# One-hot matrices kept in DRAM, and a last layer that fetches its source rows by indirect transfer

## The chip, the cores and the metric

The kernel runs on one core of one Trainium2 chip. The metric is the device time of one execution in microseconds, measured without the profiler; 27495.0 us is the median of three runs before the change. Times of stages and instructions come from one further execution that the hardware profiler recorded.

The core's engines run side by side and meet at semaphores: PE (matrix products; its weight loads are counted as PEld), DVE (vector operations), ACT (activations and copies), POOL (simple elementwise work, and the issue of indirect transfers) and SP (issue of ordinary transfers). A product written with fp32 operands is carried out as two passes, which the trace shows as two records.

## What is computed

Four graph layers over 12500 nodes of 16 features and 412500 edges (`src`, `dst`, a type of eight, 16 edge attributes), each followed by a residual and a layer norm:

```python
m = segment_sum(einsum('emh,eh->em', A[edge_type], x[src]), dst)      # layer 0, then a GRU cell
m = segment_sum(einsum('ei,eio->eo', x[src], efeat @ We + be), dst)   # layer 1
h = segment_sum((x[src] @ W[edge_type]) * norm, dst) + x @ root + b   # layer 2, twice (2a, 2b)
# layer 3: both ends of an edge are mixed and their messages are added at both ends
xs, xd = x[src], x[dst]
reflection = lambda a, b: relu(concat([a, b]) @ W1.T + b1) @ W2.T + b2
F_s, F_d = householder(reflection(xs, xd)), householder(reflection(xd, xs))
L_sd = -einsum('eki,ekj->eij', F_s, F_d)
coef = deg_inv_sqrt[src] * deg_inv_sqrt[dst]
msg_s = coef * einsum('eij,ej->ei', L_sd, xd)
msg_d = coef * einsum('eji,ej->ei', L_sd, xs)
out = relu(x - zeros.at[src].add(msg_s) - zeros.at[dst].add(msg_d))
```

Everything is fp32 at the interface. Layer 3 needs, for every edge, the row of its source and of its target, each plain and scaled by the node's inverse root degree (`dis`).

## The kernel before

**Sorting.** `sorted_path` first writes a record of 20 numbers per edge (place of the target in its block, place of the source in its block, a three-bit code `lo`, type, attributes) into a DRAM table `rb`, with 3223 indirect transfers of 128 records each (L1158), and counts degrees with one-hot products meanwhile. After that the edges lie in 100 blocks of targets (`NDB`, 125 nodes each), and within a block in 13 cells by group of sources (`NS`), two to four tiles of 128 edges each, 39 tiles (`TB`) in all. All later stages go through these 1300 cells in order.

**The pipeline of a layer.** `Layer.run` goes through the cells, one iteration per cell, and calls three stages on three neighbouring cells: the first stage on cell i, the second on cell i-1, the third on cell i-2. `prepare` asks at fixed cells of a block for what the next blocks need (records at cell 3, the column arrays `hi` and `lo` at cell 0, one-hots of sources at cells 8 to 10), and `after` puts work into later iterations. Every engine executes its part in the order in which it was written; nothing reorders it. All ordinary transfers of a layer are issued by SP.

The first stage gathers source rows on PE: `gather` multiplies the node table, split in three bf16 parts, by a one-hot of the source's place (L1264), and DVE keeps the right eighth of the result with `lo` (L1266). It also makes the one-hots of targets: `targets` has POOL compare, tile by tile, a row of 0 to 124 with each edge's place (L1275) and write a 128 x 125 fp32 matrix. The second stage folds the gathered rows (products with `fold`, L1346, L1489) and multiplies them by type or attribute on DVE (L1358, L1492). The third adds them up over the block's edges with the one-hot of targets as an operand of an fp32 product (L1382, L1506). So layers 0, 1, 2a and 2b each make the same 3900 target matrices anew, in four buffers `target`.

In layer 2a, `by_type` is also given `dis_tab`: beside each gather a further product fetches the sources' `dis` values (L1334), ACT copies them (L1339), PE turns them (L1349) into the same PSUM tile as the folded rows, ACT copies that part out (L1354), and at the end of a block DVE selects and stores them in `dis_e` (L1397 to L1402). Layer 3 reads `dis_e`.

**Layer 3.** `rows3` gathers the source rows as above and makes, on POOL, a second one-hot `to_d` the other way round (L1666). `hidden` forms the hidden layer for both directions with two fp32 products 128 to 512 columns wide (L1685, L1686) and a Relu on ACT. `ends` turns things back to one edge per partition with three products per tile (second weight matrix, source row, scaled target row; L1698 to L1700) and copies them out. Once a block is complete, `reflections` computes its two Householder reflections in fourteen steps over the whole block, two of them on POOL (L1731, L1732), the others mostly on DVE. After that come the sums: `put_cell` makes one-hots `from_s` of the source's place on POOL and adds the messages to the source's accumulators (L1791); `put_block` makes all 39 target one-hots of the block in one iteration and adds up the messages at the targets (L1801):

## Time and profile before

| | us |
|---|---|
| runs before, median (lowest, highest) | 27495.0 (27483.48, 27551.82) |
| profiled execution, its own time | 27450.57 |
| span of its instructions | 27448.7 |
| busy: PE, PEld | 23153.0, 19061.4 |
| busy: DVE, ACT, POOL | 14425.5, 2855.9, 20842.0 |
| granted TensorE clock, mean | 0.853 of full |
| moved by DMA | 1347.76 MB, 49 GB/s over the span |

A busy engine is one with an instruction under way; for PE, whose products overlap in a pipeline, that is more than its work at full rate. The stages stand one after another in the trace: the sort and its preparation until 5296 us, layer 0 until 8080, layer 1 from 8097 to 11535, layer 2a from 11590 to 16001, layer 2b from 16020 to 18600, layer 3 from 18650 to 27410; small node-wise steps lie between them. The clock is what the chip grants TensorE over time; in this trace it is either full or half, so a mean of 0.82 over a stage says that about a third of the stage ran at half clock.

In the lists of groups, a line gives engine, operation, what is written and read, sizes and count; then the busy time in us and the mean of one in ns; then the idle time of the engine just before these instructions, and what ended it.

### The profile page before, as it was taken

The page shows a single profiled execution, that of the slowest core. Times are in us where ns is not written, and L with a number is a line of the kernel's source. Part 1 is how long each engine was busy: PE and PEld are TensorE (multiplying, and loading weights), DVE is VectorE, ACT ScalarE, POOL GpSimd, SP SyncE. Part 2 cuts the span into 40 slices and gives each one's busy share as a digit, 9 for nine tenths or more (in the row PEclk, how much of TensorE's full clock was granted, in tenths as well). Part 3 has the DMA queues.
Part 4 walks back from the last instruction along what each step waited for, and adds up shares of the span by engine and source line. Part 5 has one row for each costly group of instructions (what it writes and reads, how often), then busy time and mean ns, then how long its engine had stood idle before and what let it go on. Part 6 is the DMA issues. An engine that isn't in the chain of part 4 may idle for free.

```text
span 27448.7 us, 382621 instructions
## 1 busy us (share of the span) xinstructions
PE 23153.0 (84%) x143679; PEld 19061.4 (69%) x143679; DVE 14425.5 (53%) x31460; ACT 2855.9 (10%) x8264; POOL 20842.0 (76%) x28149
## 2 busy tenths in 40 slices
PE   1666400299999999999999999998999999999998
PEld 0444300288878888777777778887888888888887
DVE  7999700166666666644444466664334344344433
ACT  0000000000001111122211200001111111111111
POOL 3888777798876666555554579996888888888888
PEclk9999855599999999987776799998888888888887
DMA  2000111133322222211111123331111111111100
GB/s 81 12 12 12 13 15 15 35 92 85 84 75 68 68 68 68 58 58 54 51 51 48 54 75 91 91 91 39 33 35 35 35 35 35 35 35 35 34 31 23
DMA packets 799013, 1347.76 MB, mean 49 GB/s; under 512 B 537098, under 2 KB 588689, under 8 KB 732485
## 3 DMA queue, kind: packets, MB, share of 16 engines
q1 hardware_dynamic: 676142, 1268.61, 16.6%
q0 software_dynamic: 103136, 33.21, 0.8%
q8 instruction: 1150, 18.84, 0.3%
q10 hardware_dynamic: 17883, 21.35, 0.2%
q14 instruction: 702, 5.75, 0.1%
HBM read 1245.07 MB, written 77.79 MB: 48 GB/s over the span
## 4 chain that ended last, share of the span: by engine, by line
PE 69%; POOL 18%; DMA 5%; issue 4%; DVE 3%; ACT 0%; another core or an unknown queue 0%; SPq 0%; POOLq 0%; ACTq 0%; DVEq 0%
POOL rb L1158 13%; PE g L1264 11%; PE acc L1382 10%; PE x L1346 8%; PE g L1801 8%; PE acc L1506 7%; DMA rec<-rb 4%; PE acc_s L1791 4%; PE hid_ps L1685 3%; PE hid_ps L1686 3%; PE ends_ps L1700 3%; PE ends_ps L1699 3%; POOL target L1275 3%; PE ends_ps L1698 3%; PE x L1489 3%
## 5 line engine op out<-in xcount | busy, mean ns | idle before, releaser
L1275 POOL TENSOR_SCALAR target<-iota_f,rec 128x125 f32<-128x125 f32 x19500 | 11698.1, 624 | 3872.9 <-PE acc L1382 2537.4
L1266 DVE SCALAR_TENSOR_TENSOR masked<-lo,part_lo,g 128x384 f32<-128x384 uint8 (+2 forms) x6500 | 3991.1, 614 | 8807.2 <-PE g L1264 8759.7
L1264 PE MATMUL g<-oh,table 125*128 125x384 bf16 (+2 forms) x19500 | 4635.2, 349 | 124.7 <-DVE oh L1245 124.3
L1158 POOL DMA_INDIRECT rb<-rec,at x3223 | 3692.2, 1146 | 1074.0 <-issue 981.8
L1382 PE MATMUL acc<-target,pr 128*128 128x125 f32 x23400 | 3962.1, 310 | 0.0
L1346 PEld LDWEIGHTS x<-fold,masked 128*128 128x128 f32 x23400 | 3377.5, 210 | 512.4 <-issue 268.4
L1346 PE MATMUL x<-fold,masked 128*128 128x16 f32 x23400 | 3337.7, 270 | 16.0 <-DVE masked L1266 16.0
L1382 PEld LDWEIGHTS acc<-target,pr 128*128 128x128 f32 x23400 | 3266.2, 211 | 35.6
L1275 POOL TENSOR_SCALAR from_s<-iota_f,rec 128x125 f32<-128x125 f32 x3900 | 3263.2, 855 | 11.4 <-PE acc_s L1791 10.6
L1358 DVE TENSOR_TENSOR pr<-x,w 128x384 f32<-128x384 f32 (+2 forms) x3900 | 2172.6, 557 | 1385.2 <-ACT d_e L1354 1282.4
L1264 PEld LDWEIGHTS <-table 125*128 125x128 bf16 x19500 | 2025.6, 105 | 934.9 <-issue 242.3
L1172 PE MATMUL cnt_ps<-in_col,in_row 128*125 128x400 bf16 x6446 | 1608.9, 330 | 915.4 <-DVE in_col L1147 600.7
L1801 PE MATMUL g<-msg,target 128*125 128x16 f32 x7800 | 2249.5, 379 | 1.0 <-POOL target L1275 0.3
L1666 POOL TENSOR_SCALAR to_d<-jd,part 125x384 f32<-125x384 uint8 (+2 forms) x1300 | 1678.7, 1291 | 746.0 <-PE ends_ps L1700 637.9
L1801 PEld LDWEIGHTS g<-msg,target 128*125 128x125 f32 x7800 | 1926.7, 308 | 323.9 <-POOL target L1275 3.9
L1506 PE MATMUL acc<-pr,target 128*125 128x272 f32 x7800 | 2106.5, 406 | 0.0
L1045 PE MATMUL tp<-ident,x_rows 125*128 125x125 f32 x13 | 5.6, 462 | 2053.5 <-DMA x_rows<-in_x 2051.3
L1172 PEld LDWEIGHTS <-in_row 128*125 128x125 bf16 x6446 | 857.9, 133 | 1261.7 <-issue 643.6
L1698 PEld LDWEIGHTS ends_ps<-w,hid 128*128 128x128 f32 x7800 | 1323.1, 196 | 389.8 <-issue 119.2
L1506 PEld LDWEIGHTS acc<-pr,target 128*125 128x125 f32 x7800 | 1364.8, 188 | 216.9 <-issue 0.3
L1791 PE MATMUL acc_s<-placed,from_s 128*125 128x128 f32 x7800 | 1306.8, 305 | 219.2 <-POOL from_s L1275 209.5
L1699 PE MATMUL ends_ps<-fold,masked 128*128 128x16 f32 x7800 | 1483.5, 266 | 0.0
(301 smaller groups left out, 28568.6 us busy)
## 6 DMA issues: line engine op xcount, KB each, us to landing
hi<-hi_d SPq DMA_DIRECT2D x500, 1218.8 KB
lo<-lo_d SPq DMA_DIRECT2D x500, 624.0 KB
rec<-rb SPq DMA_DIRECT2D x500, 390.0 KB
jd<-jd_d SPq DMA_DIRECT2D x100, 609.4 KB
rb<-rec,at POOLq DMA_INDIRECT x3223
rec<-in_edge_attr SPq DMA_DIRECT2D x100, 256.0 KB
rb<-null SPq DMA_DIRECT2D x7, 3030.0 KB
rb<-null ACTq DMA_DIRECT2D x6, 3030.0 KB
```

The costliest lines, as they stand in the source:

```text
L1158: put = nc.gpsimd.indirect_dma_start(out=rb, out_offset=bass.IndirectOffsetOnAxis(ap=at[:, t : t + 1], axis=0), in_=rec[:, k, :], in_offse ...
L1172: nc.tensor.matmul(cnt_ps[:NB, h, :NC2], in_row, in_col[:, h * NC2 : (h + 1) * NC2], start=False, stop=False, skip_group_check=True,)
L1264: nc.tensor.matmul(g[:, :w], tab[:NB, s, k, :], self.oh[d][:NB, cols], start=k == 0, stop=k == 2)
L1266: nc.vector.scalar_tensor_tensor(m[:, :w], self.lo[d][:, cols], part_lo, g[:, :w], op0=OP.is_equal, op1=OP.mult)
L1275: nc.gpsimd.tensor_scalar(oh[:, k, :], iota_f[:, :NB], self.rec[d][:, t + k, code : code + 1], None, op0=OP.is_equal)
L1346: nc.tensor.matmul(x[:, k, :D], m[:, k * P : (k + 1) * P], fold, start=True, stop=True)
L1358: nc.vector.tensor_tensor(pr[:, :n], x[:, :n, None, :D].to_broadcast([P, n, R, D]), layer.w8[d][:, t : t + n, :, None].to_broadcast([P, n, ...
L1382: nc.tensor.matmul(acc[:, :NB], pr[:, k].rearrange("p r f -> p (r f)"), oh[:, k, :], start=t + k == 0, stop=t + k == TB - 1,)
L1506: nc.tensor.matmul(acc[:NB, :WE], oh[:, k, :], pr[:, k, :], start=t + k == 0, stop=t + k == TB - 1)
L1699: nc.tensor.matmul(ps[:, k, 2 * D : 3 * D], m[:, here], fold, start=True, stop=True)
L1791: nc.tensor.matmul(acc_s[:NB, s // 4, s % 4, :], oh[:, k, :], placed[:, k].rearrange("p l f -> p (l f)"), start=False, stop=False, skip_gr ...
L1801: nc.tensor.matmul(ps[:NB, :D], oh[:, k, :], msgs[d][:, t + k, 1, :], start=t + k == 0, stop=t + k == TB - 1,)
```

## The change

**Target one-hots are made once.** `targets` becomes `make`, which has POOL make a cell's matrices as before, now in six buffers, and has SP write them to DRAM, and `fetch`, which loads a cell's matrices from DRAM. Layer 0 makes and stores the targets (`to_d`, 100 arrays of 128 x 4875 fp32). Layers 1, 2a and 2b load them, seven cells at the start and then one cell per iteration, six cells ahead, into ten buffers. Layer 1 also makes and stores the one-hots of sources (`from_d`). The stores and loads of a three-tile cell have 192 KB.

**Layer 2a loses the side product**: `dis_tab`, `d24` and `dis_e` go, and so 2a runs the same instructions as 2b.

**Layer 3 is written anew.** A DRAM table `pairs` holds each node's row beside its scaled row, 32 numbers. `fetch_sources` has POOL fetch, per tile, the 128 rows of the edges' sources with one indirect transfer, nine cells ahead, at addresses that DVE computes from the records. The targets' rows, plain and scaled and each in three bf16 parts, come from one product per tile with a bf16 one-hot `to_t` (made by DVE, three operations a block), and DVE adds the three parts. A tile's two rows stand side by side, one transpose per cell turns them (`turn_rows`), and one fp32 product per tile gives the hidden layer (`hidden`). `ends` keeps one product per tile. The sums take both one-hots from DRAM and add target messages cell by cell; POOL makes no one-hots here. `idle` issues products of zeros into a spare part of PSUM: five an iteration of 384 columns, twenty in every 52nd. The loop is written out; the stages of a cell lie one iteration apart, and its sums come 30 iterations after its rows. The loads of `hi` and `lo` and the table go from this layer; `jd` becomes bf16 (1.2 MB a block in place of 0.6).

```diff
+        def make(self, d, t, n, code, to, name):
+            oh = self.work.tile([P, 4, NB], F32, name=name, bufs=6)
             for k in range(n):
                 nc.gpsimd.tensor_scalar(
                     oh[:, k, :], iota_f[:, :NB], self.rec[d][:, t + k, code : code + 1], None, op0=OP.is_equal
                 )
+            nc.sync.dma_start(to[d][:, t * NB : (t + n) * NB], oh[:, :n, :].rearrange("p t j -> p (t j)"))
             return oh
+        def fetch(self, j, of, name="target", bufs=10):
+            d, s, t, n = all_cells[j]
+            oh = self.work.tile([P, 4, NB], F32, name=name, bufs=bufs)
+            nc.sync.dma_start(oh[:, :n, :].rearrange("p t j -> p (t j)"), of[d][:, t * NB : (t + n) * NB])
+            self.fetched[name, j] = oh
...
             while i < n + len(stages) - 1 or any(j >= i for j in self.later):
+                if ahead is not None:
+                    for j in range(0 if i == 0 else i + 6, i + 7):
+                        ahead(j)
...
             def rows(i, d, s, t, n, _):
                 m = layer.gather(d, s, t, n)
-                d24 = None
-                if dis_tab is not None:
...
-                return m, layer.targets(d, t, n), d24
+                if first:
+                    return m, layer.make(d, t, n, 0, to_d, "target")
+                return m, layer.fetched.pop(("target", i))
...
         def rows1(i, d, s, t, n, _):
-            return layer.gather(d, s, t, n), layer.targets(d, t, n)
+            layer.make(d, t, n, 1, from_d, "from")
+            return layer.gather(d, s, t, n), layer.fetched.pop(("target", i))
...
+        def idle(n):
+            for _ in range(n):
+                nc.tensor.matmul(
+                    side[:, :3].rearrange("p b c -> p (b c)"), zeros[:, :P], zeros[:, : 3 * P], start=True, stop=True
+                )
+        def targets_t(d, k):
+            w = TB * P // 3
+            cols, to = to_t[d]
+            here = slice(k * w, (k + 1) * w)
+            nc.vector.tensor_scalar(to[:NB, here], cols[:NB, here], part[:NB], None, op0=OP.is_equal)
+        def fetch_sources(j):
+            d, s, t, n = all_cells[j]
+            if s == 0:
+                ends_of[d] = work.tile([P, TB, 5, D], F32, name="ends", bufs=3)
+            for k in range(t, t + n):
+                nc.gpsimd.indirect_dma_start(
+                    out=ends_of[d][:, k, 2:4, :].rearrange("p k f -> p (k f)"), out_offset=None,
+                    in_=pairs, in_offset=bass.IndirectOffsetOnAxis(ap=at_of[d][:, k : k + 1], axis=0),
+                )
...
+        def rows3(i, d, s, t, n):
+            ps = psum.tile([P, 4, 3 * 2 * D], F32, name="rows_ps", bufs=1)
+            for k in range(n):
+                nc.tensor.matmul(
+                    ps[:, k, :], to_t[d][1][:NB, (t + k) * P : (t + k + 1) * P],
+                    x_parts[d][:NB].rearrange("p k c -> p (k c)"), start=True, stop=True,
+                )
+            return ps
+        def sum_rows(j, ps, d, t, n):
+            x_of[j] = work.tile([P, 4, 2, D], F32, name="x_e", bufs=3)
+            parts = ps[:, :n, :].rearrange("p t (k c f) -> p c t f k", k=3, f=D)
+            nc.vector.tensor_reduce(x_of[j][:, :n, 0, :], parts[:, 0], AX.X, OP.add)
+            nc.vector.tensor_reduce(ends_of[d][:, t : t + n, 4, :], parts[:, 1], AX.X, OP.add)
+            nc.scalar.copy(x_of[j][:, :n, 1, :], ends_of[d][:, t : t + n, 2, :])
...
+        def put(j):
+            d, s, t, n = all_cells[j]
+            placed = put_of.pop(j)
+            to, oh = layer.fetched.pop(("target", j)), layer.fetched.pop(("from", j))
+            sums = acc_s[:, 3].rearrange("p s c -> p (s c)")[:NB, (2 + d % 2) * P : (2 + d % 2) * P + D]
+            for k in range(n):
+                nc.tensor.matmul(
+                    sums, to[:, k, :], msgs[d][:, t + k, 1, :], start=False, stop=False, skip_group_check=True
+                )
...
         with tc.manual_schedule():
-            layer.run([rows3, hidden, ends], prepare3)
+            for i in range(n_cells + late_by):
...
+                fetch_sources(i + LEAD)
+                j = i - late_by + 6
+                if 0 <= j < n_cells:
+                    layer.fetch(j, to_d, bufs=8)
+                    layer.fetch(j, from_d, "from", bufs=8)
...
+                idle(5 if i % (4 * NS) else 20)
```

## The prediction

> **What bounds the kernel now.** I read the page's table and slices first, then a table of windows by stage, then each stage's groups and waits.
>
> ```profile
> span 27448.7 us, 382621 instructions
> ...
> POOL 3888777798876666555554579996888888888888
> ...
> PEclk9999855599999999987776799998888888888887
> ```
>
> No engine bounds the whole: POOL (76% busy) and PE (84%) change places, and the clock granted to PE is below full in the middle and at the end. By stage (sorting, layer 0, layer 1, layer 2a, 2b, layer 3; the columns after the length are busy us of PE, PEld, DVE, ACT, POOL, then clock, DMA share, GB/s):
>
> ```profile
> 0.00:5296.00 5296.00, 1781.83 (x9797) 1311.38 (x9797) 3103.99 (x13050) 84.28 (x442) 3853.45 (x3249) 0.80 0.12 22
> 5296.00:8080.00 2784.00, 2649.83 (x20077) 2399.63 (x20077) 1736.88 (x3047) 105.30 (x437) 2351.00 (x3910) 0.93 0.31 84
> 8097.00:11535.00 3438.00, 3433.05 (x20406) 2797.79 (x20405) 2251.37 (x3003) 352.92 (x1614) 2305.98 (x3887) 1.00 0.24 67
> 11590.00:16001.00 4411.00, 4280.55 (x25073) 3151.60 (x25073) 2013.65 (x3490) 921.85 (x2708) 2419.22 (x3887) 0.76 0.17 52
> 16020.00:18600.00 2580.00, 2468.23 (x19906) 2265.46 (x19907) 1746.87 (x3202) 30.68 (x114) 2361.58 (x3900) 0.98 0.33 90
> 18650.00:27410.00 8760.00, 8506.75 (x48302) 7116.17 (x48302) 3503.77 (x5609) 1327.76 (x2899) 7540.93 (x9300) 0.82 0.11 34
> ```
>
> All but the first run over 100 target blocks, so the lengths are also us per block times 100: 27.8, 34.4, 44.1, 25.8, 87.6. Layer 1 is PE alone (busy 3433 of 3438 at clock 1.00). 2a and 2b compute the same thing from different tables; 2a carries the `d24` side product as well and takes 1.7 times as long, at clock 0.76. Layer 3 is POOL, 7541 of 8760 busy, with one-hot matrices:
>
> ```profile
> L1275 POOL TENSOR_SCALAR from_s<-iota_f,rec 128x125 f32<-128x125 f32 x3900 | 3263.2, 855 | 11.4 <-PE acc_s L1791 10.6
> L1275 POOL TENSOR_SCALAR target<-iota_f,rec 128x125 f32<-128x125 f32 x3900 | 2250.5, 618 | 0.0
> L1666 POOL TENSOR_SCALAR to_d<-jd,part 125x384 f32<-125x384 uint8 x1108 | 1433.7, 1294 | 606.9 <-PE ends_ps L1700 590.5
> ```
>
> In each block `put_block` makes 39 targets in one run of 22.5 us (timeline of POOL) while PE follows at POOL's pace. In 2a the waits are those of the side product, not of POOL, which itself waits for PE:
>
> ```profile
> POOL target L1275 <- PE acc L1382: 1998.9, 1272, 20.2
> DVE pr L1358 <- ACT d_e L1354: 1280.3, 1200, 3.5
> ```
>
> 2b shows PE's own pace at full clock, from one gather to the next (1.82 us for a cell of three tiles):
>
> ```profile
> 17100.63 0.65 PE L1264 MATMUL g<-oh,table 125*128 125x384 bf16 x3
> 17101.12 0.74 PE L1346 MATMUL x<-fold,masked 128*128 128x16 f32 x6
> 17101.71 0.91 PE L1382 MATMUL acc<-target,pr 128*128 128x125 f32 x6
> 17102.45 0.65 PE L1264 MATMUL g<-oh,table 125*128 125x384 bf16 x3
> ```
>
> Each fp32 product is two passes, started 0.112 us apart, whatever its width up to 128 columns; a bf16 one of 384 columns takes 0.163 us.
>
> **The change, part by part.** Against this profile's 27448.7 us (execution 27450.6; the median of the runs, 27495, lies 44 us above).
>
> *2a loses the side product.* 1300 products of L1334, 3900 of L1349, two ACT copies per cell, the wait 1280 us, and the end-of-block work of L1397 to L1402 go. What remains is 2b's program, for which 2b is the row: 2580. PE by its pace: 13 x 1.82 = 23.7 us a block, plus about 1.3 for `by_f` and `node`: 25.0, against POOL's 23.6 now. So 2b was nearly PE-bound already, and freeing POOL in it is worth at most 0.8 us a block, which I give to late transfers. 2a: 4411 to 2600, **-1811**; 2b: 2570, **-10**. The cover is the clock: were 2a granted layer 0's 0.93, it would be 2600/0.93 = 2800.
>
> *Layer 0 stores each target matrix.* POOL still makes 39 a block (23.5). A cell's buffer is now free when PE has used it and its 192 KB store has landed; six buffers replace four. The nearest row for a landing behind other traffic is the column load at 2b's start:
>
> ```profile
> 16022.28 0.34 SPq L1236 DMA_DIRECT2D hi<-hi_d  x1
> ...
> 16035.97 1.78 DVE L1245 TENSOR_SCALAR oh<-hi,part 125x1664 bf16<-125x1664 bf16 x3 [17.55 <-DMA hi<-hi_d]
> ```
>
> 13.7 us from issue to use. By the packet records its 9984 B packets (0.376 us) run on about five of the sixteen DMA engines. The stores stand in SP's queue behind this load once a block, and in the order of instructions each SP transfer also waits for the eighth before it to land. Six cells last 6 x 2.0 = 12 us; a store behind `hi` lands some 16 us after it, so POOL may stall 4 us a block: 0 to +400 us, below nothing too (two more buffers): -100. I take **+120**, as POOL has some slack (23.5 of 27.8). Queued behind SP's wait for POOL are the loads of `rec`, `hi`, `lo`, needed 8 cells later.
>
> *Layer 1 loads targets and stores `from`.* PE-bound; POOL's 39 makes (23.1 of 34.4) and the loads lie beside it; what comes onto SP is 26 issues of 0.33 us. The ten `target` buffers give a load 9 cells x 2.5 = 23 us against 16 us of landing. **+20**; ends 0 and +250 (a queue at 2.5 us a block).
>
> *2a, 2b load targets* beside PE: 9 cells x 1.82 = 16.5 us against the same 16, covered with nothing to spare; if not, +2 us a block each (+400).
>
> *Layer 3.* POOL's 75.4 busy us a block go. What comes onto POOL is 39 indirect gathers a block; before has scatters of the same 128 rows:
>
> ```profile
> 2499.47 1.33 POOL L1158 DMA_INDIRECT rb<-rec,at  x1 [0.30 <-issue]
> ...
> 4000.77 0.96 POOL L1158 DMA_INDIRECT rb<-rec,at  x1 [0.30 <-issue]
> ```
>
> Start to start they come every 1.26 us with VectorE silent and every 1.64 us while VectorE compares without a break. So POOL needs 39 x 1.26 = 49.1 to 39 x 1.64 = 64.0 us a block. VectorE's share: of its work in layer 3 only the long operations with two SBUF operands (L1744, L1751, L1757, L1763, L1765, L1769: 5 x 1.45 + 2 x 0.82 = 8.9 us) and the compares of `targets_t` (3 x 0.65) hold POOL up; overlaps with `from_s` show it: 0.60 us undisturbed, 0.86 on average. By the scatters' rate (0.38 us lost in 1.64) those 10.8 us cost 2.5 us; blocked outright, 10.8. I take 4: **53 us a block**, nearer the scatters, the same instruction.
>
> PE at full clock, per block: `sums`, `acc_s`, `hidden`, `ends` 4 x 39 x 0.224 = 34.9; `turn_rows` 13 x 0.22 = 2.9; `rows3` 39 x 0.08 = 3.1 (between L1349's 0.04 and a 256-column gather's 0.113); dummy products 65 x 0.163 = 10.6: **51.5 us**. DVE: 13 x (`add_bias` 0.2 by L1392, two reductions 0.25 each by L1737's 1.15 ns an element, `at_lo` 0.2, `placed` 0.69) = 20.7, reflections 14.4, compares and small ones 3.5: 38.6. ACT about 15; its copy of a gathered row waits for the gather, and behind it stand the copies and the Relu that PE needs, which nine cells of lead cover. SP takes over 28 issues of 0.33 us, 9 us of a block in which it was idle. DMA: 26 matrices of 192 KB, `jd`, records and rows, 7 MB a block, 130 GB/s over 54 us; 2b moves 90, and three 390 KB record loads at its start ran at 190 (packet records). PE's `put` waits for two transfers, asked for six cells (25 us) ahead. POOL at 53 and PE at 51.5, coupled through nine cells of lead: 54.5 us a block. Ends: 51.5 and 64. Plus start (table `pairs`, first gathers) 45 and the drain of 30 cells at about 2.2 us, 65: 100 x 54.5 + 110 = 5560, **-3200**.
>
> The gap before 2a loses its table, **-15**. Sum: 120 + 20 - 1811 - 10 - 3200 - 15 = -4896: 27451 to 22555. The median stands 0.16% above the profiled execution; with that, **22590**.
>
> Row first, then page: L1275's `from_s` at 855 ns against `target`'s 618 in the same stage is VectorE standing in POOL's way. The Trainium skill, "GPSIMD Engine Reference", Key points, says that POOL shares its SBUF interfaces with VectorE, in contention with two-port modes or two SBUF inputs; by that rule, taken fully, the sum would be 23140 in place of 22590. Row: the sort's scatters of 10 KB follow each other at 1.26 us. Against that speaks the Trainium skill, "DMA: Bandwidth & Descriptors", Anatomy of one DMA: a transfer issued from POOL costs 2.0 us plus its bytes at 436 GB/s. An estimate by it is 2.04 us for a gather of 16 KB, 79.5 us a block were each to wait for the last, and a sum of 25100; the row is below it since eight are in flight, and I go by the row.
>
> **The rivals.**
> 1. *VectorE blocks the gathers*: 49.1 + 10.8 = 60 us a block, 100 x 60 + 110 = 6110, 550 over my term: 23140 (at 64 us: 23540). For it: the `from_s` row. Against it: scatters lost only 0.38 us beside a fully busy VectorE. 14%.
> 2. *Late transfers bind layers 0 to 2*: layer 0 at 32 us (+300 on my term), layer 1 +130, 2a and 2b +2 us a block each (+400): 23420. For it: 13.7 us landings and one queue. Against: DMA share 0.33 at most. 10%.
> 3. *The clock falls*: layer 3 at 0.82, as now, 51.5/0.82 = 62.8 us (+830), 2a at 0.93 (+200): 23620. For it: 2a lost its clock with PE 97% busy. Against: layer 1 and 2b hold 0.98 to 1.00 and layer 3 has no 22 us stretch at POOL's pace left. 8%.
> 4. *Landings pace the gathers, slower than before.* Each gather waits for the eighth before it to land. Landing at 13.7 us means 1.71 us each, 67 us a block (+1230), 23820 (4%). Level with before is reached only when layer 3 takes 8760 + 1696 = 10456, or 103 us a block: 2.65 us a gather, 21 us per landing; past that it is slower. Against it: 1.26 us steady in the sort bounds the landing there by 10 us. 4%.
>
> **How the numbers follow.** The forecast, 60%: 22000 to 23100 (layer 3 at 50 to 58 us, layer 0 at 27 to 30). The rivals as above, the two cases of the fourth together 8%. The range 21900 to 24000 leaves out the slower end of the fourth and tails. Faster by over 0.3% (about what a measurement here can tell from no change) 0.95, same 0.01, slower 0.04.
>
> **What will show it.** 2a's window equal to 2b's within 5%, clock 0.97 or more; layer 1 within 2%; layer 0's POOL waiting for DMA stores, if my +120 is right; in layer 3 POOL's gathers 1.3 to 1.45 us apart, PE busy above 90%, clock near 1.00. Wrong if the gathers come over 1.6 us apart, if PE waits for `target` or `from` transfers, or if layer 2 stays at 40 us a block.

## The result: slower on the chip of the record, and the profile after

The changed kernel took 27992.2 us (median; 27965.5 to 28024.0), beside 27523.4 us for the kernel before in the same series (27483.5 to 27553.3). The ratio is 1.0172, with a 95% interval of 1.0151 to 1.0192. The forecast was 22590 us. The profiled execution took 27974.95 us, its span is 27972.9 us.

The stages (us). So that they add up, each layer is taken from its first gather product (L1264 before, L1267 after) to that of the next layer, and layer 3 from the last gather product of 2b to the end. The forecast is before's length plus the terms of the sum, with the -15 for the gap counted in layer 1. The last column is the same changed kernel on another chip, run at the end of the study:

| stage | before | forecast | after | after, chip 4 |
|---|---|---|---|---|
| sort | 5327 | 5327 | 5329 | 5327 |
| layer 0 | 2769 | 2889 | 3346 | 3341 |
| layer 1 | 3487 | 3492 | 3490 | 3490 |
| layer 2a | 4455 | 2644 | 2596 | 2597 |
| layer 2b | 2552 | 2542 | 2565 | 2570 |
| layer 3 | 8860 | 5660 | **10647** | **5532** |
| span | 27449 | 22553 | 27973 | 22856 |

Layer 3 is the step that failed, by 4987 us on this chip and by 128 us the other way on chip 4. Layer 0 came out 457 and 452 us over the forecast.

The page of the changed kernel, its span and the slices of POOL and of TensorE's granted clock:

```profile
span 27972.9 us, 376773 instructions
...
POOL 3888777667776676710000001333333333333332
PEclk9999855677779999999999999677766666666666
```

POOL is idle through layer 2 and only a third busy in layer 3, the last sixteen slices. The clock, full in layers 1 and 2, falls to 0.6 with layer 3. The table of windows (layers 0, 1, 2a, 2b, 3, with bounds a little within or beyond the stages': those of 2a and 2b open 25 and 54 us after the first gather product; after the length, busy us of PE, PEld, DVE, ACT, POOL, then clock, DMA share, GB/s):

```profile
5296.00:8600.00 3304.00, 3116.79 (x20011) 2806.83 (x20012) 1706.53 (x3002) 91.25 (x417) 2323.77 (x3900) 0.78 0.46 147
8646.00:12110.00 3464.00, 3430.08 (x20404) 2796.13 (x20404) 2271.76 (x3008) 352.44 (x1613) 2382.98 (x3900) 0.99 0.71 211
12190.00:14725.00 2535.00, 2445.66 (x19741) 2245.95 (x19739) 1704.64 (x3171) 30.62 (x114) 0.00 (x0) 0.99 0.72 187
14815.00:17331.00 2516.00, 2427.87 (x19654) 2231.70 (x19652) 1696.96 (x3157) 29.44 (x111) 0.00 (x0) 0.99 0.72 187
17345.00:27930.00 10585.00, 6535.08 (x43447) 5759.16 (x43444) 3543.78 (x9291) 1401.17 (x4206) 3730.65 (x3900) 0.67 0.28 70
```

In layer 3 no engine is near full: PE 62%, DVE 33%, POOL 35%, the DMA engines 28%. So everybody waits. The table of waits of layer 3 (engine, line, whom it waited for: total us, times, longest):

```profile
ACT x_t L1732 <- PE side L1728: 3332.9, 1058, 6.7
DVE ends L1752 <- remote: 2428.2, 138, 41.2
ACT x_t L1732 <- remote: 1740.6, 135, 52.1
...
ACT sum_d L1837 <- remote: 1470.5, 86, 34.9
PE side L1639 <- issue: 1185.3, 138, 41.7
```

"Remote" and "issue" mean that the profile shows nobody who released the wait in time. `add_bias` (L1752) waits for nothing but TensorE's products of L1747, yet 138 of its waits, up to 41 us long, are put down to nobody. The timeline of one such stretch shows why:

```profile
21985.74 0.27 PE L1728 MATMUL side<-ident,x_e 128*96 128x128 f32 x1
...
21986.52 0.53 PE L1747 MATMUL ends_ps<-w,hid 128*128 128x32 f32 x4
...
21989.49 0.94 POOL L1684 DMA_INDIRECT ends<-pairs,at_i  x1 [0.30 <-issue]
21989.75 0.26 ACT L1732 COPY x_t<-side 96x128 f32<-96x128 f32 x1 [6.26 <-remote]
21990.07 0.97 PE L1639 MATMUL side<-zeros 128*128 128x384 bf16 x5 [3.02 <-issue]
21990.74 0.95 POOL L1684 DMA_INDIRECT ends<-pairs,at_i  x1 [0.30 <-issue]
...
21991.01 0.93 PE L1833 MATMUL acc_s<-msg,target 128*125 128x16 f32 x4
...
21997.46 0.23 DVE L1752 TENSOR_TENSOR ends<-ends_ps,b 128x64 f32<-128x64 f32 x1 [9.80 <-remote]
...
22017.07 0.17 ACT L1837 COPY sum_d<-acc_s 125x16 f32<-125x16 f32 x1 [23.08 <-remote]
...
22017.44 1.22 PE L1840 MATMUL acc_s<-placed,from 128*125 128x128 f32 x4 [25.51 <-issue]
```

The transpose L1728 is over at 21986.0, and ScalarE, which waits for nothing but TensorE and its own earlier work, copies it at 21989.75: 3.7 us late. The products of L1747 end at 21987.05 and VectorE takes them at 21997.46, 10.4 us late. Those of L1833 end at 21991.94 and `sum_d` follows at 22017.07, 25 us late. Meanwhile POOL issues a gather every 1.25 us, undisturbed. Each gather is as cheap as hoped; what is late is the news that TensorE is done. TensorE itself has gone on to later products by then (L1639 at 21990.07, L1833 at 21991.01). The ends of products are modelled in these records, though, so results that reach PSUM late would look the same.

The trace also records raises of semaphores. For each recorded raise of TensorE's in layer 3 I took the time since the end of the last product recorded before it, and sorted the raises by how long POOL's run of gathers had been going (a run is 39 gathers, 49 us, then POOL waits some 57 us for the next free `ends` tile):

```
us since the run of gathers began    raises   median lateness us   95th percentile
 0 to 5                                 667         0.01                 0.12
 5 to 10                                291         0.09                 3.23
10 to 15                                164         1.82                 4.43
20 to 25                                 61        11.0                 13.8
35 to 40                                 33        22.8                 26.3
55 to 60                                761         0.01                22.4
65 to 110                              5802         0.01                 0.01
VectorE's raises, all of layer 3       7669         0.01                 0.02 (longest)
```

The lateness grows as long as gathers go and is gone a few us after the run. VectorE's recorded raises are never late. Not every raise left a record: of VectorE's in the first 50 us of the runs, 737 of 1906 did. The waits say the same without these records. Between 5 and 50 us into a run, 89% of TensorE's 222 waits of over 1 us end within 0.35 us of the end of an instruction of ScalarE or VectorE; only 12% of ScalarE's 319 and 35% of VectorE's 317 end so soon after an instruction of the other two. So it is TensorE's news that is late. In the sort, where POOL scatters every 1.26 us, those of TensorE's raises that left a record are 0.02 us late at most; the same holds for layers 0 to 2 (medians 0.01 us, at most 0.02 us in 99% of them). That much the profile of the changed kernel says; what sets it off needed runs.

### The profile page after: what moved, and what is told of

It reads as the page before. It is cut to its first block, busy times and chain, and to the rows that moved or that the text cites. A ratio compares the mean times of both kernels' runs of the same rounds, so it can differ in the third digit from the quotient of the medians.

```text
span 27972.9 us, 376773 instructions
## 1 busy us (share of the span) xinstructions
PE 19864.6 (71%) x133626; PEld 17244.4 (62%) x133626; DVE 14144.4 (51%) x34826; ACT 2023.8 (7%) x6956; POOL 12293.8 (44%) x14949
## 5 line engine op out<-in xcount | busy, mean ns | idle before, releaser
L1684 POOL DMA_INDIRECT ends<-pairs,at_i x3900 | 3730.6, 957 | 11931.5 <-DMA w_h<-in_l_w_t 5300.4
L1269 DVE SCALAR_TENSOR_TENSOR masked<-lo,part_lo,g 128x384 f32<-128x384 uint8 (+2 forms) x5200 | 3192.4, 614 | 3868.1 <-PE g L1267 3769.0
L1382 PE MATMUL acc<-target,pr 128*128 128x125 f32 x23400 | 3850.4, 304 | 0.0
L1267 PE MATMUL g<-oh,table 125*128 125x384 bf16 (+2 forms) x15600 | 3626.6, 343 | 116.2 <-DVE oh L1248 116.2
L1382 PEld LDWEIGHTS acc<-target,pr 128*128 128x128 f32 x23400 | 3214.4, 208 | 0.3
L1840 PE MATMUL acc_s<-placed,from 128*125 128x128 f32 x7800 | 1494.6, 339 | 2088.8 <-issue 1557.8
L1278 POOL TENSOR_SCALAR from<-iota_f,rec 128x125 f32<-128x125 f32 x3900 | 2383.0, 632 | 1106.7 <-DMA from_d<-from 1037.0
L1639 PE MATMUL side<-zeros 128*128 128x384 bf16 x7060 | 1722.2, 387 | 1548.5 <-issue 1185.3
L1278 POOL TENSOR_SCALAR target<-iota_f,rec 128x125 f32<-128x125 f32 x3900 | 2323.8, 615 | 997.5 <-PE acc L1382 635.7
L1840 PEld LDWEIGHTS acc_s<-placed,from 128*125 128x125 f32 x7800 | 1243.2, 236 | 2093.8 <-issue 1559.7
L1752 DVE TENSOR_TENSOR ends<-ends_ps,b 128x96 f32<-128x96 f32 (+2 forms) x1300 | 334.0, 257 | 4066.0 <-remote 2428.2
L1267 PEld LDWEIGHTS <-table 125*128 125x128 bf16 x15600 | 1600.0, 103 | 780.4 <-issue 195.4
L1639 PEld LDWEIGHTS <-zeros 128*128 128x128 bf16 x7060 | 840.7, 131 | 1998.9 <-issue 1799.1
L1739 PE MATMUL hid_ps<-x_t,w_h 96*128 96x128 f32 (+2 forms) x7800 | 1420.4, 331 | 218.2 <-ACT hid L1741 167.4
```

Source lines behind the costliest of these rows:

```text
L1267: nc.tensor.matmul(g[:, :w], tab[:NB, s, k, :], self.oh[d][:NB, cols], start=k == 0, stop=k == 2)
L1269: nc.vector.scalar_tensor_tensor(m[:, :w], self.lo[d][:, cols], part_lo, g[:, :w], op0=OP.is_equal, op1=OP.mult)
L1278: nc.gpsimd.tensor_scalar(oh[:, k, :], iota_f[:, :NB], self.rec[d][:, t + k, code : code + 1], None, op0=OP.is_equal)
L1382: nc.tensor.matmul(acc[:, :NB], pr[:, k].rearrange("p r f -> p (r f)"), oh[:, k, :], start=t + k == 0, stop=t + k == TB - 1,)
L1639: nc.tensor.matmul(side[:, :3].rearrange("p b c -> p (b c)"), zeros[:, :P], zeros[:, : 3 * P], start=True, stop=True)
L1684: nc.gpsimd.indirect_dma_start(out=ends_of[d][:, k, 2:4, :].rearrange("p k f -> p (k f)"), out_offset=None, in_=pairs, in_offset=bass.Indi ...
```

## The experiments

The results name the chip of each group of runs; for the record of the changed kernel itself no chip is named. Layer 3's us a block are the mean distance of the `sum_d` copies (L1837), the last three distances, in which the pipeline drains, left out. "Late" is the share of TensorE's raises in layer 3 over 1 us late; in the changed kernel it is 9.9%, at 104.7 us a block.

### Chip 7: without the gathers, paced, unread, and the other way round

`e1_plain`: the gathers give way to one plain transfer a block.

```diff
                 ends_of[d] = work.tile([P, TB, 5, D], F32, name="ends", bufs=3)
-            for k in range(t, t + n):
-                nc.gpsimd.indirect_dma_start(
-                    out=ends_of[d][:, k, 2:4, :].rearrange("p k f -> p (k f)"), out_offset=None,
-                    in_=pairs, in_offset=bass.IndirectOffsetOnAxis(ap=at_of[d][:, k : k + 1], axis=0),
-                )
+                nc.scalar.dma_start(
+                    ends_of[d][:, :, 2:4, :].rearrange("p t k f -> p t (k f)"),
+                    pairs[: P * TB].rearrange("(t p) c -> p t c", p=P),
+                )
```

> Layer 3 as in the changed kernel, but the 39 indirect gathers of a block are replaced by one plain transfer of the same bytes in the same 128 B pieces, issued by ScalarE; the rows that arrive are not those of the edges' sources, so the sources' terms are left out of the computation. In the changed kernel layer 3 takes 10585 us (105 us a block), and TensorE's semaphore updates come up to 39 us after the recorded end of the product that makes them, only while POOL's gathers run. Theory A (the gathers, as indirect transfers of POOL's own queue, delay what TensorE reports as done): layer 3 falls to 51 to 56 us a block, 5200 to 5700 us, whole kernel about 22900 to 23100, updates on time. Theory B (SP's queue starves TensorE: the loads of the stored one-hot matrices and of the 1.22 MB target columns land late, whoever loads the sources): layer 3 stays at 95 to 110 us a block, whole kernel 27000 to 28000. Theory C (any transfer of 4992 pieces of 128 B a block into SBUF does it): layer 3 also stays above 80 us a block.

22454 us; 49.5 us a block, 0.0% late. The window of layer 3:

```profile
17345.00:22430.00 5085.00, 4952.59 (x43523) 4451.86 (x43523) 3536.47 (x9305) 1415.21 (x4220) 0.00 (x0) 0.99 0.60 145
```

The same products, at clock 0.99 and PE 97% busy: theories B and C fall on this chip. SP's queue, the loads of `target` and `from` and 4992 pieces of 128 B a block hurt nothing here.

`e1_paced`: POOL waits in each iteration for ScalarE.

```diff
             nc.scalar.copy(x_t_of[j][: n * 2 * D], tp[: n * 2 * D])
+            tick[j] = work.tile([P, 1], F32, name="tick", bufs=8)
+            nc.scalar.copy(tick[j][:64], x_t_of[j][:64, :1])
...
+                if i - 2 in tick:
+                    pace = work.tile([P, 1], F32, name="pace", bufs=2)
+                    nc.gpsimd.tensor_copy(pace[:64], tick.pop(i - 2)[:64])
                 fetch_sources(i + LEAD)
```

> The changed kernel with a pace for POOL: each iteration ScalarE copies one column of the turned rows to a small tile, and POOL copies it before it issues that iteration's three gathers, so the 39 gathers of a block come three an iteration instead of 39 in one run of 49 us. Theory A1 (the delay builds only in a long uninterrupted run of gathers: it is under 0.1 us in the first 5 us of a run and over 10 us after 20 us): layer 3 falls to 55 to 65 us a block, whole kernel 23000 to 24200. Theory A2 (each gather costs TensorE its time wherever it stands, about 1.25 us x 39 = 49 us a block on top of 52): layer 3 stays at 95 to 110 us a block, whole kernel 27000 to 28500. Theory B (SP's queue): layer 3 stays too.

23084 us, 55.2 us a block, 0.0% late: as A1 had it. I took this for the cure; the later groups take that reading away.

`e1_unread` and `e1_scatter`: plain transfers as above, and POOL's 3900 transfers into nothing.

```diff
+                    at_fix = work.tile([P, TB], I32, name="at_fix", bufs=1)
+                    nc.vector.tensor_scalar(at_fix, iota_f[:, :TB], float(P), part, op0=OP.mult, op1=OP.add)
...
-                    out=ends_of[d][:, k, 2:4, :].rearrange("p k f -> p (k f)"), out_offset=None,
+                    out=spares[d][:, k, :, :].rearrange("p k f -> p (k f)"), out_offset=None,
```

> As e1_plain (the sources' rows are left out, plain transfers in their place), but POOL issues its 3900 indirect gathers as well, all in one run from the start of layer 3, into tiles that nobody reads and with fixed addresses, so nothing waits for them. They last 3900 x 1.25 = 4875 us; after that layer 3 goes on without gathers, so one run shows both. Theory A (gathers delay TensorE by running, not by being waited for): while they run a block takes 110 us or more, so about 35 to 45 blocks are done in 4875 us, the rest at 51 to 56 us, layer 3 about 7900 to 8700 us, whole kernel 25400 to 26200. Theory D (the stalls come from waiting for the gathered rows): 51 to 56 us a block throughout, layer 3 5200 to 5700, whole kernel about 23000.

> As e1_unread, but POOL's 3900 indirect transfers go the other way: 128 rows of 128 B from SBUF scattered to DRAM rows that nobody reads, as the sort stage does (there TensorE's updates are 0.01 us after the recorded ends, beside 1.26 us scatters). The sources' rows are left out. Theory A as it stands for any indirect transfer: same as e1_unread, layer 3 7900 to 8700 us. Theory A with the direction (only rows that come from DRAM into SBUF delay TensorE): 51 to 56 us a block, layer 3 5200 to 5700 us.

22790 and 22834 us; both 49.5 us a block while gathers or scatters came every 1.37 and 1.38 us, 0.0% late. So a run of indirect transfers need not delay TensorE. Theory A as I had stated it was gone.

### Chip 2: runs without readers, one pace a block, another pace, a fourth buffer

```diff
 e2_bursts_unread (e1_unread with the blocks' own addresses)
-                    in_=pairs, in_offset=bass.IndirectOffsetOnAxis(ap=spares["at"][:, k : k + 1], axis=0),
+                    in_=pairs, in_offset=bass.IndirectOffsetOnAxis(ap=at_of[d][:, k : k + 1], axis=0),
 e2_pace_block (e1_paced, once a block)
-                if i - 2 in tick:
+                if i - 2 in tick and (i + LEAD) % NS == 0:
 e2_pace_dve (the changed kernel, and)
+            at_c = work.tile([P, 4], I32, name="at_c", bufs=4)
+            nc.vector.tensor_copy(at_c[:, :n], at_of[d][:, t : t + n])
...
-ap=at_of[d][:, k : k + 1]
+ap=at_c[:, k - t : k - t + 1]
 e2_ends4 (the changed kernel, and)
-name="ends", bufs=3) ... name="at_i", bufs=3)
+name="ends", bufs=4) ... name="at_i", bufs=4)
```

> As e1_unread (the sources' rows come by plain transfers from fixed rows, so their terms are left out), but the gathers use each block's own addresses, as in the changed kernel, so POOL is held once a block until the addresses of the block after next are made: runs of 39 gathers with a wait between, into tiles that nobody reads. Theory E (a run of 39 gathers that starts after a wait delays TensorE's updates whoever reads them): layer 3 stays at 90 to 110 us a block, whole kernel 26500 to 28000. Theory F (the delay needs somebody who waits for the gathered rows, ScalarE's copy and VectorE's products, beside POOL running ahead): 53 to 57 us a block, whole kernel 22700 to 23100.

> e1_paced with POOL's pacing copy only once a block, ahead of the block's first gather, so the 39 gathers again come in one run of 49 us, nine cells ahead of their use, and are read as in the changed kernel. Theory F or E (the run of 39 is what does it): layer 3 goes back to 90 to 110 us a block, whole kernel 26500 to 28000. Theory G (what matters in e1_paced is that POOL no longer waits for the release of the ends tile itself, not how the gathers are spread): 54 to 57 us a block, about 23100.

> The pace of e1_paced made another way: in each iteration VectorE copies that iteration's three addresses to a small tile of their own, and the gathers read them there, so they wait for VectorE and POOL executes nothing but gathers; ScalarE's extra copy is gone too. If the spreading is what helps: 54 to 57 us a block, whole kernel 22950 to 23150. If it was POOL's copy between the gathers (an instruction of another kind that breaks the run): 90 to 110 us a block, 26500 to 28000.

> The changed kernel with four instead of three buffers for the tile the rows land in, and four for the addresses: POOL no longer waits for the release of the tile but for the addresses, and each run of 39 gathers starts some nine iterations earlier, its rows landing long before ScalarE copies them. Theory H (the runs come too late: ScalarE waits for rows, TensorE behind it, and the loop falls out of step): 55 to 65 us a block, whole kernel 23000 to 24200. Theory E or F (the run of 39 itself): 90 to 110 us a block, 26500 to 28000.

27557, 27992, 25274 and 27695 us; 100.8, 105.3, 77.6 and 101.5 us a block; 9.0, 9.3, 7.8 and 9.8% late. `e2_bursts_unread` says that nobody need wait for the gathered rows (theory F falls) and `e2_ends4` that the runs are not too late (theory H falls). `e2_pace_block` says that one wait of POOL's own does not help (theory G falls). The pace through VectorE helps by half. Its layer 3, window and two waits:

```profile
17345.00:25220.00 7875.00, 7052.27 (x43468) 6170.43 (x43467) 3641.03 (x10587) 1393.20 (x4208) 3876.49 (x3900) 0.71 0.37 94
```

```profile
POOL ends L1686 <- DVE at_c L1684: 1504.2, 508, 7.7
POOL ends L1686 <- DVE ends L1754: 1010.3, 229, 9.1
```

POOL now waits for VectorE in most iterations, so gathers come in threes; PE is busy 7052 us where `e1_plain` needed 4953, at clock 0.71. Compared with `e1_unread`, `e2_bursts_unread` differed in its program only in the addresses and in the wait for them, and so the next runs vary these; that it ran on another chip I left out of account.

### Chip 14: addresses, layout, a copy on POOL, and layer 0

```diff
 e3_unread_rows (e1_unread, and)
-                    nc.vector.tensor_scalar(at_fix, iota_f[:, :TB], float(P), part, op0=OP.mult, op1=OP.add)
+                    nc.vector.tensor_copy(at_fix, at_of[0])
 e3_blockmajor (the changed kernel, and)
-        nc.sync.dma_start(pairs[: P * NPB].rearrange("(p n) c -> p (n c)", p=P), both)
+        nc.sync.dma_start(
+            pairs[: P * NPB].rearrange("(n p) c -> p n c", p=P), both.rearrange("p (n c) -> p n c", c=2 * D)
+        )
...
-                at, layer.rec[d][:, :, 1], float(NPB), eight_s[:, d // LO, :], op0=OP.mult, op1=OP.add
+                at, eight_s[:, d // LO, :], float(P), layer.rec[d][:, :, 1], op0=OP.mult, op1=OP.add
...
-            nc.vector.tensor_add(at_of[d], at, lo_e[d])
+            nc.vector.scalar_tensor_tensor(at_of[d], lo_e[d], float(P), at, op0=OP.mult, op1=OP.add)
 e3_pool_copy (e1_paced without ScalarE's tick)
-                if i - 2 in tick:
+                if i >= 2:
-                    nc.gpsimd.tensor_copy(pace[:64], tick.pop(i - 2)[:64])
+                    nc.gpsimd.tensor_copy(pace[:64], part[:64])
 e3_paced_early (e1_paced, and)
-            if k == 3 and d and d + 2 < NDB:
-                layer.load_records(d + 2)
+            if k == (0 if first else 3) and d and d + 2 < NDB:
+                layer.load_records(d + 2, 4 if first else 3)
```

> e1_unread with one difference: the 3900 unread gathers, all in one run without a wait on another engine, use the addresses of the first block's edges (rows scattered over the table, as in the changed kernel) instead of rows p + 128 k, which lie one behind the other. The sources' rows are again left out of the computation. Theory J (what delays TensorE is a run of gathers of scattered rows; rows in sequence do not do it): while the gathers run TensorE does about 4 cells in 49 us, as inside a run of the changed kernel, so about 30 blocks in 4875 us and 70 blocks at 49 us after: layer 3 about 8300 us (7500 to 9500), whole kernel 24900 to 26900. Theory K (the waits between runs do it, the addresses do not): 49 to 51 us a block as in e1_unread, whole kernel 22700 to 22900.

> The changed kernel with the table of pairs laid out by block (row block x 128 + j instead of j x 104 + block), so the rows of one cell lie in 128 KB instead of being spread over 1.7 MB; runs of 39 gathers as before, no pace. Theory J in the form that nearness is what counts: 50 to 60 us a block, whole kernel 22500 to 23600. Theory J in the form that only rows in sequence are harmless, or theory K: 90 to 110 us a block, 26500 to 28000.

> e1_paced without the pace: POOL copies a constant column before each iteration's three gathers and waits for nobody, so runs of 39 gathers stay, broken every third gather by an instruction of another kind (e2_pace_dve had the pace without the copy: 78 us a block). If the copy is what helps in e1_paced: 54 to 60 us a block, whole kernel 22900 to 23600. If the pace is: 85 to 110 us a block, 26000 to 28000. Both in part: 65 to 85 us a block.

> e1_paced, and in layer 0 the records of the block after next are loaded three cells earlier (ahead of the two column loads, with a fourth buffer). In the changed kernel TensorE waits 175 us in layer 0 for these records (55 waits, up to 9.9 us), which stand on SP's queue behind stores that wait for POOL, and its clock is 0.78 there. If that wait is what costs layer 0 its 520 us: layer 0 falls from 3304 to 2800 to 2950 us, whole kernel 22550 to 22800. If the stores cost it otherwise (SP's queue or the columns' loads late): layer 0 stays above 3200 us, whole kernel 23000 to 23150.

22790, 22903, 23017 and 22814 us; 49.5, 53.6, 55.1 and 55.0 us a block; 0.0% late in all four. `e3_paced_early`, over four executions, has a ratio of 0.8319 (0.8292 to 0.8345) to the kernel before. Theory J fell with `e3_unread_rows`, whose scattered rows did no harm; theory K was left. But `e3_blockmajor` was free of the delay with the changed kernel's instructions in the changed kernel's order. Either its addresses or the form of one VectorE instruction had to matter, or something outside the program.

### Chip 6: the changed kernel again, one instruction's form, another pitch, and the layout again

```diff
 e4_stt
-            nc.vector.tensor_add(at_of[d], at, lo_e[d])
+            nc.vector.scalar_tensor_tensor(at_of[d], lo_e[d], 1.0, at, op0=OP.mult, op1=OP.add)
 e4_pitch
-    pairs = dram.tile([(P + 1) * NPB, 2 * D], F32, name="pairs")
+    pairs = dram.tile([P * (P + 1), 2 * D], F32, name="pairs")
...
-                at, layer.rec[d][:, :, 1], float(NPB), eight_s[:, d // LO, :], op0=OP.mult, op1=OP.add
+                at, layer.rec[d][:, :, 1], float(P), eight_s[:, d // LO, :], op0=OP.mult, op1=OP.add
 e4_blockmajor_early: e3_blockmajor with e3_paced_early's two lines of layer 0
 e4_again: no edit
```

> The changed kernel once more, unchanged. e3_blockmajor and e2_bursts_unread say that two kernels with the same instructions in the same order can take 54 or 100 us a block, so it has to be known whether the state is the kernel's or the run's. If the kernel's: 27900 to 28100 us in every execution, as measured before (27965 to 28024). If chance decides: an execution near 23000 us among them.

> The changed kernel with one VectorE instruction of a block written in the form that e3_blockmajor has there (the addresses' second addition as a multiply by 1 and add); the table and the addresses stay j x 104 + block. If the addresses are what made e3_blockmajor fast (theory J): 27800 to 28200 us, as the changed kernel. If that form of instruction or its timing is what did it: 22800 to 23200 us.

> The changed kernel with the table of pairs at a pitch of 128 rows for each j in place of 104 (row j x 128 + block, 16 KB from one j to the next in place of 13 KB): the rows of a tile are scattered as widely as before, only at other distances. Theory J (wide scatter is what delays TensorE): 90 to 110 us a block, 26500 to 28500 us. If only the distance of 13312 B does it, or the state hangs on details of timing: 53 to 57 us a block, 22800 to 23300 us.

> The two repairs together: the table laid out by block as in e3_blockmajor and layer 0's records loaded three cells earlier as in e3_paced_early (which gave 270 us, 23084 to 22814). Expected: 22903 less 270, 22600 to 22700 us, a ratio of 0.823 to 0.828 to the kernel before. If e3_blockmajor's speed was chance: back near 27700 us.

27986 (27957 and 28014), 28022, 28039 and 27767 us (27714 to 27843); 104.0 to 104.8 us a block and 9.6 to 10.0% late in all four. `e4_blockmajor_early` has a ratio of 1.010 (1.007 to 1.013) to the kernel before. The layout that was free of the delay on chip 14 has it here, with the same instructions in layer 3. The instruction's form and the pitch make no difference. What had gone together all along was the group, and with it the chip.

### Chip 4: the changed kernel as a marker, and the paced one beside it

> The changed kernel once more, as a marker of the chip. e4_blockmajor_early (27767 us) has e3_blockmajor's layer 3 (22903 us) instruction for instruction, and the two were on different chips; in all four calls every kernel with unpaced runs of gathers from its own blocks' addresses was slow together or fast together. Theory L (the chip, or what else is on it, decides whether runs of gathers delay TensorE): 27900 to 28100 us on a chip like those of the second and fourth call, 22800 to 23100 us on one like those of the first and third, where this kernel has not been. Theory M (each kernel's own program decides): 27900 to 28100 us on any chip.

> e3_paced_early unchanged, beside the marker. On a chip where the marker takes 22800 to 23100 us: 22800 to 22830 us as before, nothing new. On a chip where the marker takes 28000 us: 22800 to 22850 us if POOL's copy that waits for ScalarE cures the delay there too (e2_pace_dve, paced without that copy, took 25274 us on such a chip); 25000 to 28000 us if the pace helps only in part or not at all.

The changed kernel, not a line altered, took 22858 and 22882 us: a ratio of 0.8326 (0.8301 to 0.8350) to the kernel before. `e5_paced_early` took 22836 and 22843 us, 0.8314 (0.8290 to 0.8339). Theory L holds and M falls. The page and the windows of layers 0 and 3 of `e5_after`:

```profile
POOL 2788877776776775676661000000004777777775
PEclk9999985556787779999999999999998999999998
```

```profile
5296.00:8600.00 3304.00, 3102.23 (x20028) 2788.88 (x20029) 1709.93 (x3009) 92.54 (x419) 2316.81 (x3900) 0.79 0.46 147
...
17345.00:22813.00 5468.00, 5259.19 (x43443) 4712.41 (x43444) 3538.59 (x9290) 1407.45 (x4205) 4149.29 (x3900) 0.93 0.53 135
```

Layer 0 takes 3257 us from its first gather product to its last, against 3262 on the chip of the record; layer 3's window has 5468 us in place of 10585, PE 96% busy. Its timeline in the middle of a run of gathers:

```profile
20001.48 0.27 PE L1728 MATMUL side<-ident,x_e 128*96 128x128 f32 x1
...
20001.85 0.26 ACT L1732 COPY x_t<-side 96x128 f32<-96x128 f32 x1 [2.54 <-PE side L1728]
20002.17 0.95 POOL L1684 DMA_INDIRECT ends<-pairs,at_i  x1 [0.30 <-issue]
...
20003.42 0.94 POOL L1684 DMA_INDIRECT ends<-pairs,at_i  x1 [0.30 <-issue]
20004.67 0.94 POOL L1684 DMA_INDIRECT ends<-pairs,at_i  x1 [0.30 <-issue]
...
20005.92 1.54 POOL L1684 DMA_INDIRECT ends<-pairs,at_i  x1 [0.30 <-issue]
```

The copy of the turned rows starts 0.10 us after the transpose is over, beside gathers at the same 1.25 us; the waits on "remote" are gone and 0.0% of the raises are late. The kernel before shows no such difference: 27344 to 27575 us on all the chips.

The kept traces tell the two kinds of chip apart even in the sort, which is the same code in every kernel and takes as long on all of them (layer 0's first product of L1382 starts at 5329 to 5338 us). TensorE makes 6485 semaphore raises there. In every run on chips 7, 14 and 4 all of them left a record; in every run on chips 2 and 6, and in the profiles of the record before and after, only 3387 to 3400 did, and of VectorE's some 13025 only 10583 to 10760. In layers 0 to 2, without indirect transfers, next to none is missing on either kind. So the chip of the record is of the kind of 2 and 6, and chip 7 of the other. This takes the weight off the first group: `e1_plain` and `e1_paced` never met the delay, and no run without gathers was made where it occurs. Against theory B there, the profile after itself speaks: in layers 1 to 2b the transfers of SP keep the DMA engines busier (0.71 to 0.72, against 0.28 in layer 3), and no recorded raise of TensorE's is over 0.02 us late.

`e5_paced_early` is for layer 0 a comparison on one chip, `e5_after` being beside it. Its layer 0, window and two waits:

```profile
5296.00:8400.00 3104.00, 2944.25 (x20052) 2653.23 (x20052) 1723.85 (x3022) 96.87 (x427) 2330.16 (x3900) 0.83 0.50 156
```

```profile
POOL target L1278 <- DMA to_d<-target: 516.0, 78, 9.8
...
PE acc L1382 <- POOL target L1278: 129.5, 53, 6.2
```

From its first gather product to its last, layer 0 takes 3051 us here, 3257 in `e5_after` and 2689 in the kernel before: the records' lateness cost 206 of the 568 us. What is left, 362 us, I put down to the stores: POOL waits 516 us for them and PE then for POOL. No run left them out, so this is not shown. In layer 3 the pace costs 2.0 us a block (55.4 against 53.4), so on such a chip it is a loss that the gain in layer 0 covers.

## Why the prediction was right and wrong

**Layer 3, "coupled through nine cells of lead: 54.5 us a block": right on chip 4, wrong on the chip of the record.** On chip 4 it took 53.4 us a block and 5468 us by its window, against 54.5 and 5560. POOL's term holds: gathers on average 1.369 us apart, 53.4 us a block, against 53. I had put VectorE's share at 4 us: 53.4 less 39 x 1.25 = 48.8 makes it 4.6. The row above shows it: the gather at 20005.92 took 1.54 us in place of 0.94, and from 20005.19 to 20006.64 the trace has VectorE in a product of two SBUF tiles (L1799). Over the layer, the 1055 gathers that overlap one of VectorE's long operations on two SBUF tiles take 1.36 us in the mean and the other 2845 0.95, which makes 4.3 of the 4.6 us. The Trainium skill, "GPSIMD Engine Reference", Key points, says that POOL shares its SBUF interfaces with VectorE and that the two contend when VectorE has two inputs in SBUF. The trace agrees in kind, with 4.6 us a block where the rule taken fully made it 10.8. By the Trainium skill, "DMA: Bandwidth & Descriptors", Anatomy of one DMA, a gather was estimated at 2.04 us. The trace has 1.25 us from one to the next, as a gather need not wait for the one before. PE's term was 51.5 and `e1_plain` has 49.5 us without any gathers. PE was busy 96%, as I had asked for; its clock was 0.93 and not near 1.00.

On the chip of the record the failing words are the ones that couple the two engines. They took for granted that an engine's finished work is known at once to those who wait for it. There TensorE's raises came up to 41 us late during POOL's runs. ScalarE and VectorE waited, TensorE waited for them, and its clock fell: each of its 299 stops of over 2 us in this layer lies in a stretch at half clock or is followed by one. Of the 5117 us between the two layers 3, TensorE's busy time has 1276 (6535 less 5259, the same products at a lower clock) and its idle time the other 3841.

**The fourth rival** named the right price and the wrong thing. It put break-even at 103 us a block, and the record has 105. But it wanted gathers 2.65 us apart. Over a whole block they are 2.69 us apart, the wait between runs included; inside the runs they came at 1.25 us, and POOL waited for the others. The check that I had listed, "wrong if the gathers come over 1.6 us apart", would have pointed at POOL. The other, "if PE waits for `target` or `from` transfers", did not occur either.

**Layers 2a and 2b: right.** 2a has become 2b's program: from the first gather product to the last, 2552 and 2565 us, against 2600 and 2570, at clock 0.98 to 0.99. From the first gather product of 2a to the last of 2b the gain is 1845 us (7006 less 5161) against 1821 forecast. The small term for 2b had the wrong sign: 13 us more in place of 10 less.

**Layer 1: right.** With the gap behind it, +3 us against +20 - 15.

**Layer 0, "I take +120": undersized, beyond my end of +400.** From its first gather product to its last it took 573 us more (3262 against 2689), and 568 more on chip 4. I had POOL stall behind its stores, and it does; but I gave the loads on SP's queue "needed 8 cells later" no price. The waits of the changed kernel's layer 0:

```profile
POOL target L1278 <- PE acc L1382: 635.7, 483, 5.6
POOL target L1278 <- DMA to_d<-target: 290.0, 48, 7.5
...
PE codes_t L1231 <- DMA rec<-rb: 175.2, 55, 9.9
```

The records are asked for three cells ahead of the transposes that read them (L1231), behind stores that wait for POOL. One such stop, and a gather product (L1267) before and after it:

```profile
7423.56 0.65 PE L1267 MATMUL g<-oh,table 125*128 125x384 bf16 x3
...
7431.70 0.87 PE L1231 MATMUL codes_t<-ident,rec 128*39 128x128 f32 x3 [6.15 <-DMA rec<-rb]
7432.36 1.17 PE L1267 MATMUL g<-oh,table 125*128 125x384 bf16 x3
```

Here too the clock falls with the stops: all 50 stretches at half clock in this layer begin within 4 us of a stop of over 1 us, and the median one lasts 27 us. Most stops are shorter than this one, 2 to 4 us. Of the 573 us, 492 are TensorE's busy time (3106 less 2614, the same products) and 80 its idle time. The clock went from 0.93 to 0.78; blocks often lie 27 and 37.5 us apart in turn, the longer one with the stop. I had priced POOL's stall by its length and left out the clock.

**The sum.** On chip 4 the span is 22855.8 us against 27449 less 4896 = 22553: +452 for layer 0, -2 for layer 1, -47 for 2a, +28 for 2b and -128 for layer 3. My range held it. On the chip of the record the range failed, since no case in it had one chip differ from another.

**What stays open.** Shown is that one and the same program takes 22858 to 22882 us on chip 4 and 27957 to 28014 on chip 6. Every changed kernel on chips 2 and 6 had the delay, and all had gathers in layer 3; nothing on 7, 14 and 4 had it. That the gathers set it off is read from the phase of the lateness within their runs, and from `e2_pace_dve`, which spread them and halved the loss. What it is about the chip, or about what else was on it at the time, no run tells; nor why TensorE's raises alone are late, and the sort's scatters harmless. The packets of the transfers took as long on both kinds (medians of 44 ns for the gathers' queue and 64 ns for SP's). The missing records leave one rival that nobody tested: that the recording itself delays TensorE there. Every execution on record has a granted clock beside its time, so none is known to have run unrecorded. Whether `e1_paced`'s pace cures a slow chip was not tried on one. On a slow chip the best kernel seen is `e2_pace_dve`, 25274 us in one execution against 27378 for the kernel before; on the others `e3_paced_early` and the changed kernel itself lie within 0.3% of each other, at 0.83.

## What to carry to other kernels

When many waits are put down to nobody ("remote", "issue") and the engines named had long been done, compare the end of the work with the start of what waits for it, before looking for a busy engine. Run the unaltered kernel again in another group before believing that an edit cured or caused something: here the readings of the first three groups rested on comparing kernels from different chips. Compare, too, a stage that all kernels share: the count of recorded raises in the sort would have told the chips of the first two groups apart. Price a short stop of TensorE by the clock that follows it, not by its own length, and count what stands in a queue behind a transfer that must wait for a slow engine.

## What was not expected of the hardware

- TensorE's semaphore raises came up to 41 us late during runs of indirect gathers on some chips (8 to 10% of them over 1 us), and 0.02 us at most in 99% of them on others, with the same program. VectorE's recorded ones were 0.02 us late at most in 99% on both.
- On the chips with the delay, about half of TensorE's raises in the sort, beside POOL's scatters, left no record (3387 to 3400 of 6485 did), with no loss of time there; on the others all did.
- An indirect gather of 128 rows of 128 B costs POOL 0.94 us and comes every 1.25 us, whether it is read or not and whether the rows are neighbours or scattered (medians of 1.249 and 1.250 us); a scatter of the same size every 1.27.
- In layer 0 stops of TensorE of mostly 2 to 4 us were each followed by some 27 us at half clock.
